# The y images of half 0 in blocks of 16 rows and whole PSUM banks

## The chip, the cores and the metric

The kernel runs on one core of one Trainium2 chip. The metric is device time in microseconds. Before the change the median of three runs is 2890.63 us (2888.65 to 2894.42). A shorter time is better. The profile shown below is of one execution with a span of 2892.8 us.

## The reference

The program has two layers. Layer 0 is a row attention over a 256 x 256 image of 128 channels; its result x1 lies in DRAM. Layer 1 treats the 256 x 128 slices as tokens of a Fourier operator with attention. What matters here is one step of layer 1: the attention output y, a weighted sum over all tokens plus an inverse Fourier image of some modes, followed by an instance norm.

```python
attn = jnp.einsum('bats,basi->bati', probs, vh)
...
attn = fno_layer(attn, p_wr, p_wi, p_bias, p_sw, p_sb, (H, W))
attn = instance_norm(attn + tokens, attn_norm_w, attn_norm_b)
```

There are 256 tokens (two halves of 128, one token to a partition), each an image of 256 rows by 128 columns. In the kernel, y for one half is a matrix of 256 x 128 weights applied to x1 (the skip part, which has attention and identity folded into it), plus the image of the modes, scaled by a constant. The instance norm needs mean and variance over each token's whole image.

## The kernel before, in words

After the attention modes have been worked out, their intermediate `Gd0` lies in DRAM. The stage concerned here starts at 1904.5 us. The generator `y_blocks(a, psum, lo, hi)` at L1308 makes y of half `a` in units of 8 rows, 32 units to a half. Half 0 runs by itself (L1796) with eight PSUM banks; half 1 runs afterwards, woven into other work with four banks. One unit `u` does this:

- **Loads on SyncE's DMA queue.** `load(u + 2)` loads the x1 rows of the unit after next, as one tile `xt` (128 partitions x 2 x 1024 floats, two DMAs of 512 KB, L998). There are three `xt` buffers. If `u` is even it also loads the modes `gs` of a 16-row block (four DMAs of 64 KB, L1229); there are three `gs` buffers. So in the queue the modes of a block stand two units ahead of their use.
- **Skip matmuls on TensorE, L1332.** Four banks, one for each turn `j`, with two accumulating matmuls each: 128 x 128 weights `mpT` against 256 columns of `xt`. A matmul of the code shows as two MATMUL instructions in the profile, so a unit has 16.
- **Image matmuls on TensorE, L1200**, in the helper `image`. For each of two rows and each `j`, a matmul with 32 contraction rows of `gs` against `bsy`, accumulating in the same banks: 8 in the code, 16 in the profile.
- **VectorE.** Four TENSOR_TENSOR (L1342) scale the banks into `blocks`, the SBUF copy of half 0, then two BATCH_NORM_STATS2 (L1344) add the statistics.

A unit uses 256 of a bank's 512 columns, and a pool of eight banks holds two units. The order on the engines is the order of the program text: the stage stands under a manual schedule for the compute engines and SyncE. SyncE is first in, first out: a DMA whose buffer is not yet free holds up every DMA behind it. The three `xt` loads for units 0 to 2 are issued long before the stage.

```python
for j in range(4):
    for sc in range(2):
        nc.tensor.matmul(
            rows_of(ps[j]), mpT[:, sc, tt], by_turn(xt[:, sc])[:, j],
            start=(sc == 0), stop=False,
        )
image(ps, gs[b], bsy, range(2 * s, 2 * s + 2))
```

When half 0 is complete, `psy` is given back and the pool `pz` takes the banks; the norm of half 0 (bn_aggr at L1432) starts from the statistics, and half 1 begins with its own units.

Of the kernel before, what the change touches and what calls it, by code (L numbers as in the profile page):

```python
# [18 lines left out]
P = 128  # L19
# [493 lines left out]
def layer1(tc, I, C, ident, x1d, upool, U, stats2, mv2, out):  # L513
# [9 lines left out]
    with ExitStack() as ctx:  # L523
# [668 lines left out]
        def rows_of(ps):  # L1192
            return ps.rearrange("p (n w) -> p n w", w=W)
# [49 lines left out]
        def run(stage):  # L1243
            for _ in stage:
                pass
# [62 lines left out]
        def y_blocks(a, psum, lo, hi, kept=16):  # L1308

            tt = slice(a * P, (a + 1) * P)  # L1310
            gs = {}

            def load(u):
                if (a, u) not in xts:
                    xts[a, u] = load_x1(a, u)
                if u % 2 == 0:
                    gs[u // 2] = xp.tile([P, 4, P], FP, tag="gs", name=f"gs_{a}_{u}", bufs=3)
                    load_modes(gs[u // 2], Gd0, u // 2, tt)

            load(lo)  # L1320
            load(lo + 1)
            yield 0.0
            for u in range(lo, hi):
                b, s = u // 2, u % 2
                if u + 2 < hi:
                    load(u + 2)
                xt = xts.pop((a, u))
                ps = [psum.pool.tile([P, 512], FP, tag=psum.tag, name=f"yps_{a}_{u}_{j}") for j in range(4)]
                ps = [z[:, 0:256] for z in ps]
# [7 lines that stand above are left out]
                if a == 0:  # L1337
                    yt = blocks[:, b, s * HB : (s + 1) * HB]
                else:
                    yt = xp.tile([P, HB], FP, tag="yt", name=f"yt_{u}")  # L1340
                for j in range(4):
                    nc.vector.tensor_tensor(by_turn(yt)[:, j], rows_of(ps[j]), bc(rwb, 1, 2), ALU.mult)  # L1342
                for g in range(2):
                    nc.vector.bn_stats(ystat[:, a, 2 * u + g, :], yt[:, g * 512 : (g + 1) * 512])  # L1344
                if a:
                    nc.gpsimd.dma_start(ydv[:, a, u * HB : (u + 1) * HB], yt)  # L1346
                yield 4.2

        def mix_modes(mk, acc, F, l, tag, cs):

            T, G, n = P, P // 4, len(cs)
            cs = slice(cs[0], cs[0] + n)
            steps = [
                (i, x, r, dst) for i in range(4)
                for x, r, dst in ((0, "r", 0), (1, "n", 0), (0, "i", 1), (1, "r", 1))
            ]

            of = 4 // n  # L1360

            def products(k):
                made = mk("m", [P, 4, G, 4], f"{tag}m_{cs.start}_{k}")
                for q in range(of):
                    i, x, r, dst = steps[k + q]
                    f = F[:, cs, x, :].rearrange("p c (g i) -> p c g i", i=4)[:, :, :, i]
                    w = mixw[r][:, cs, 16 * l + 4 * i : 16 * l + 4 * i + 4]
                    (nc.gpsimd if (k + q) % 3 == 2 else nc.vector).tensor_tensor(
                        made[:, q * n : (q + 1) * n], bc(f, 3, 4), bc(w, 2, G), ALU.mult
                    )  # L1370
                return made.rearrange("p c g o -> p (c g o)")

            made = products(0)
            for k in range(0, 16, of):
                now = made
                if k + of < 16:
                    made = products(k + of)
                yield 0.6
                for q in range(of):
                    i, x, r, dst = steps[k + q]  # L1380
                    nc.tensor.matmul(  # L1381
                        acc[dst][:, cs.start * T : cs.stop * T], ident, now[:, q * n * T : (q + 1) * n * T],
                        start=(i == 0 and x == 0), stop=(i == 3 and x == 1),
                    )
# [408 lines left out]

        with tc.manual_schedule(engines=COMPUTE | {ENG.SP}):
            with tc.tile_pool(name="psy", bufs=8, space=PSUM) as psy:
                run(y_blocks(0, Banks(psy, "y"), 0, 32))  # L1796
            pz = _Held(tc.tile_pool(name="pz", bufs=4, space=PSUM))
            bq, br = Banks(pz.pool, "q"), Banks(pz.pool, "r")

            def tiles(wp):  # L1800
                return Tiles(F=(wp, "F", 1), f=(wp, "f", 1), m=(wp, "m", 2))

            with yctx:
                U1 = 24
                with tc.tile_pool(name="mp0", bufs=1) as wp:
                    y1 = y_blocks(1, br, 0, U1)
                    weave((2.4 * t for t in first_modes(0, wp, tiles(wp), bq, [(wp, "gt", 1)])), y1)
                    run(y1)
                with tc.tile_pool(name="hp0", bufs=2) as wp:
                    run(first_images(0, wp, xp, bq, br))  # L1810
                with tc.tile_pool(name="mp1", bufs=1) as wp:
                    y1 = y_blocks(1, br, U1, 32)
                    next(y1)
                    m0 = second_modes(
                        0, wp, tiles(wp), bq, [(xp, "xt", 3)], [(wp, "gt", 1)] * 3 + [(xp, "xt", 3)]
                    )
                    weave((2.4 * next(m0) for _ in range(3)), y1)
                    run(y1)
                    m1 = first_modes(
                        1, wp, Tiles(F=(xp, "yt", 2), f=(xp, "yt", 2), m=(xp, "gs", 3)), br, [(xp, "xt", 3)]  # L1820
                    )
                    next(m1)
                    for k, _ in enumerate(iter(lambda: next(m0), None)):
                        if k % 4 == 3:
                            next(m1)
                    for _ in m0:
                        next(m1, None)
                    o0 = output_0(bq)
                    next(o0)
                    y2 = wp.tile([P, NB], FP, tag="gt", name="y2_0", bufs=1)  # L1830
                    nc.sync.dma_start(y2, ydv[:, 1, 0:NB])
                    run(m1)
                    g2 = wp.tile([P, 4, P], FP, tag="m", name="gs2_1_0", bufs=2)
                    next(o0)
                    load_modes(g2, halves[1].Gd1, 0)
                    next(o0)
                with tc.tile_pool(name="hp1", bufs=2) as hp:
                    next(o0)
                    next(o0)
                    due, begun = 0.0, False  # L1840
                    for done in first_images(1, hp, xp, bq, br, ([y2[:, 0:HB], y2[:, HB:]], g2)):
                        if not done:
                            due += 0.9
                            begun = due > 0
                        if begun:
                            next(o0, None)
                        if done and begun:
                            due -= 1.0
                    run(o0)
            pz.release_now()  # L1850
            with tc.tile_pool(name="op1", bufs=2, side="right") as op:
                o1 = Output1(op)
                with tc.tile_pool(name="mp3", bufs=1) as wp, tc.tile_pool(
                    name="mpq3", bufs=8, space=PSUM
                ) as psq:
                    m1 = second_modes(1, wp, tiles(wp), Banks(psq, "q"), [(wp, "gt", 2)], [(wp, "gt", 2)] * 4)
                    next(m1)
                    o1.more = op
                    ahead = o1.ahead()
                    next(ahead)  # L1860
                    next(ahead)
                    next(m1)
                    next(m1)
                    next(ahead)
                    next(ahead)
                    run(iter(lambda: next(m1), 1.2))
                    run(ahead)
                    run(m1)
                with tc.tile_pool(name="opk1", bufs=8, space=PSUM) as psk, tc.tile_pool(
                    name="op2", bufs=1  # L1870
                ) as more:
                    o1.run(Banks(psk, "k"), more)
# [163 lines left out]
```

## Time and profile before

| what | value |
|---|---|
| median time | 2890.63 us |
| span of the profile | 2892.8 us |
| y of half 0 | 1904.5 to 2042.4 us |
| PE / DVE / ACT / POOL busy, whole span | 92 / 69 / 52 / 58 % |
| granted TensorE clock, whole span | 0.952 |
| L1332 `yps<-xt,mpT`, both halves | 1024 instructions, 242.9 us |
| `xt<-x1d` | 128 DMAs of 512 KB |
| `gs<-Gd` | 384 DMAs of 64 KB |

Busy time on PE is the sum of the matmuls' modelled durations; PEld is the weight loads, which overlap it; SPq is SyncE issuing DMAs. In the answers to queries, a row of windows gives length, then the busy time and instruction count of each engine, the granted TensorE clock (1.00 is full), the busy share of the DMA engines, and the bytes moved per second. A timeline row gives start, duration, engine, line, operation, tile, count, and in brackets how long the engine was idle before it and what ended the idling.

### The profile page before, as it was taken

The page shows a single profiled execution, that of the slowest core. Times are in us where ns is not written, and L with a number is a line of the kernel's source. Part 1 is how long each engine was busy: PE and PEld are TensorE (multiplying, and loading weights), DVE is VectorE, ACT ScalarE, POOL GpSimd, SP SyncE. Part 2 cuts the span into 40 slices and gives each one's busy share as a digit, 9 for nine tenths or more (in the row PEclk, how much of TensorE's full clock was granted, in tenths as well). Part 3 has the DMA queues.
Part 4 walks back from the last instruction along what each step waited for, and adds up shares of the span by engine and source line. Part 5 has one row for each costly group of instructions (what it writes and reads, how often), then busy time and mean ns, then how long its engine had stood idle before and what let it go on. Part 6 is the DMA issues. An engine that isn't in the chain of part 4 may idle for free. (4 is left out here: it accounts for less than half of the span.)

```text
span 2892.8 us, 71476 instructions
## 1 busy us (share of the span) xinstructions
PE 2653.2 (92%) x29116; PEld 1940.4 (67%) x29116; DVE 2008.2 (69%) x3263; ACT 1490.7 (52%) x2849; POOL 1682.0 (58%) x1308
## 2 busy tenths in 40 slices
PE   6799999999999999999999899999889988799654
PEld 6677777777777777777777656778665555555533
DVE  7788888888888888888888744756655545365545
ACT  0477777777777777777777622200004611365132
POOL 0399999999999999999999800200114733111211
PEclk9999999999999999999999989999999999799865
DMA  9422222222222222222222101088879983898599
GB/s 362 169 67 67 67 67 67 67 67 67 67 67 67 68 68 68 69 66 72 67 67 67 41 18 53 30 274 276 279 247 313 308 301 131 256 355 303 184 353 344
DMA packets 246705, 430.12 MB, mean 149 GB/s; under 512 B 26278, under 2 KB 174201, under 8 KB 239976
## 3 DMA queue, kind: packets, MB, share of 16 engines
q1 hardware_dynamic: 206568, 335.34, 35.2%
q0 software_dynamic: 22912, 81.80, 7.4%
q10 hardware_dynamic: 16896, 8.39, 1.0%
q8 instruction: 231, 3.78, 0.6%
q14 instruction: 98, 0.80, 0.1%
HBM read 290.17 MB, written 135.27 MB: 147 GB/s over the span
## 5 line engine op out<-in xcount | busy, mean ns | idle before, releaser
L299 POOL TENSOR_TENSOR e<-e,b1T 128x1024 f32<-128x1024 f32 x256 | 607.0, 2371 | 164.3 <-PE u L348 88.8
L303 POOL TENSOR_TENSOR es<-e 128x512 f32<-128x512 f32 x512 | 639.9, 1271 | 20.1
L281 ACT ACTIVATE sc<-sc,b2T 128x512 f32<-128x512 f32 x512 | 339.0, 662 | 365.9 <-PE sc L272 357.6
L323 DVE RECIPROCAL av<-av 128x256 f32<-128x256 f32 x256 | 452.3, 1767 | 27.2 <-DVE og L322 1.4
L281 ACT ACTIVATE e<-sc,b2T 128x512 f32<-128x512 f32 x512 | 348.7, 681 | 0.0
L294 DVE TENSOR_TENSOR e<-sc,b1T 128x1024 f32<-128x1024 f32 x256 | 310.8, 1214 | 0.0
L272 PE MATMUL sc<-qkT 32*128 32x256 f32 x4096 | 294.4, 401 | 1.3 <-DVE e L294 1.3
L311 PE MATMUL av<-e,v 128*32 128x256 f32 x4096 | 274.7, 385 | 0.5 <-POOL e L299 0.5
L1332 PE MATMUL yps<-xt,mpT 128*128 128x256 f32 x1024 | 242.9, 390 | 20.2 <-DVE yt L1342 9.3
L272 PEld LDWEIGHTS sc<-qkT 32*128 32x128 f32 x4096 | 185.6, 184 | 112.4 <-issue 97.8
L322 DVE SCALAR_TENSOR_TENSOR og<-gate,av 128x256 f32<-128x256 f32 x256 | 107.7, 421 | 191.0 <-PE av L316 191.0
L1332 PEld LDWEIGHTS yps<-xt,mpT 128*128 128x128 f32 x1024 | 192.1, 192 | 58.0 <-DVE yt L1342 12.7
L1346 POOL DMA_DIRECT2D yd<-yt x32 | 17.8, 556 | 345.8 <-DVE yt L1342 345.8
L327 POOL TENSOR_TENSOR x<-xt,bo 128x256 f32<-128x256 f32 x256 | 188.0, 734 | 0.0
L246 PE MATMUL qk<-xnT,wT_wq 128*128 128x256 f32 x512 | 179.5, 432 | 1.7 <-ACT xnT L238 1.7
L252 PEld LDWEIGHTS gv<-wT_wv,kvT 128*128 128x128 f32 x1024 | 155.0, 192 | 13.4
L316 PE MATMUL av<-es,ones 128*32 128x256 f32 x2048 | 157.5, 379 | 2.6 <-POOL es L303 2.5
L333 PE MATMUL wo<-wT_wo,og 128*128 128x128 f32 x1024 | 156.8, 276 | 2.7 <-DVE og L324 2.7
L311 PEld LDWEIGHTS av<-e,v 128*32 128x32 f32 x4096 | 107.0, 109 | 76.1 <-POOL e L299 1.0
L348 PE MATMUL u<-adft,x 128*128 128x129 f32 x1024 | 156.4, 275 | 0.0
L258 DVE COPY v<-gv 128x256 f32<-128x256 f32 x256 | 108.6, 424 | 68.6 <-PE gv L256 68.6
L252 PE MATMUL gv<-wT_wv,kvT 128*128 128x128 f32 x1024 | 156.0, 275 | 0.0
(546 smaller groups left out, 5282.2 us busy)
## 6 DMA issues: line engine op xcount, KB each, us to landing
xt<-x1d SPq DMA_DIRECT2D x128, 512.0 KB
xb<-in_x_dram SPq DMA_DIRECT2D x32, 1024.0 KB
xt<-in_x_dram SPq DMA_DIRECT2D x128, 256.0 KB
kt<-in_L_conv_kv_x_dram SPq DMA_DIRECT2D x128, 256.0 KB
x1d<-x SPq DMA_DIRECT2D x256, 128.0 KB
y<-yd SPq DMA_DIRECT2D x62, 512.0 KB
gs<-Gd SPq DMA_DIRECT2D x384, 64.0 KB
yd<-yt POOLq DMA_DIRECT2D x32, 512.0 KB, 6.2
```

Of the source, the lines that this page charges most:

```text
L246: nc.tensor.matmul(ps[:, 0:256], wT["wq"], xnT, start=True, stop=True)
L252: nc.tensor.matmul(ps[:, 256 + c * P : 256 + (c + 1) * P], kvT[:, c * P : (c + 1) * P], wT["wv"], start=True, stop=True,)
L272: nc.tensor.matmul(sc[h // 2][:, h % 2, c * 256 : (c + 1) * 256], qkT[p, 256 + c * P : 256 + (c + 1) * P], qkT[p, 0:256], start=True, stop ...
L281: nc.scalar.activation(r["e"][1][:, :, c, :] if hp else z, z, AF.Exp, bias=b2T[:, c, s : s + 1])
L294: nc.vector.tensor_tensor(r["e"][0].rearrange("p h c q -> p (h c q)"), r.pop("sc").rearrange("p h x -> p (h x)"), b1T[:, 0:2].rearrange("p ...
L299: nc.gpsimd.tensor_tensor(e1, e1, b1T[:, 2:4].rearrange("p h c q -> p (h c q)"), ALU.mult)
L303: nc.gpsimd.tensor_tensor(r["es"][hp], e[:, :, 0, :], e[:, :, 1, :], ALU.add)
L311: nc.tensor.matmul(ps[hd, 0:256], r["v"][:, c, hd], r["e"][h // 2][:, h % 2, c, :], start=(c == 0), stop=(c == 1),)
L316: nc.tensor.matmul(ps[32 * h : 32 * h + 32, 256:512], self.ones, r["es"][h // 2][:, h % 2, :], start=True, stop=True,)
L323: nc.vector.reciprocal(rd, rd)
L327: nc.gpsimd.tensor_tensor(r["x1"], r["x"], bc(self.bo, 1, 2), ALU.add)
L1332: nc.tensor.matmul(rows_of(ps[j]), mpT[:, sc, tt], by_turn(xt[:, sc])[:, j], start=(sc == 0), stop=False,)
```

## The change

Half 0 gets a function of its own, `y_half_0`. It works in 16 blocks of 16 rows. A block takes four whole banks of 512 columns; the skip matmuls of its first unit fill the first half of each bank and those of its second unit the other half, and only the first of them carries the start flag. Then all four rows' image matmuls follow at once. VectorE scales a whole bank with one TENSOR_TENSOR of 512 columns. This is meant to need fewer and larger instructions on VectorE, and fewer changes between the two kinds of matmul. At the top of a block come the loads: first `xt` of the units 2b+2 and 2b+3, then `gs` of block b itself. Half 1 stays as it was.

```diff
+        def y_half_0(psum):
+
+            tt = slice(0, P)
+            for b in range(16):
+                for u in (2 * b + 2, 2 * b + 3) if b else (0, 1, 2, 3):
+                    if u < 32 and (0, u) not in xts:
+                        xts[0, u] = load_x1(0, u)
+                gs = xp.tile([P, 4, P], FP, tag="gs", name=f"gs_0_{b}", bufs=3)
+                load_modes(gs, Gd0, b, tt)
+                ps = [psum.tile(f"yps_0_{b}_{j}") for j in range(4)]
+                for s in range(2):
+                    xt = xts.pop((0, 2 * b + s))
+                    for j in range(4):
+                        for sc in range(2):
+                            nc.tensor.matmul(
+                                rows_of(ps[j])[:, 2 * s : 2 * s + 2], mpT[:, sc, tt], by_turn(xt[:, sc])[:, j],
+                                start=(s == 0 and sc == 0), stop=False,
+                            )
+                image(ps, gs, bsy)
+                for j in range(4):
+                    nc.vector.tensor_tensor(by_turn(hb[b])[:, j], rows_of(ps[j]), bc(rwb, 1, 4), ALU.mult)
+                for g in range(4):
+                    nc.vector.bn_stats(ystat[:, 0, 4 * b + g, :], hb[b][:, g * 512 : (g + 1) * 512])
...
             with tc.tile_pool(name="psy", bufs=8, space=PSUM) as psy:
-                run(y_blocks(0, Banks(psy, "y"), 0, 32))
+                y_half_0(Banks(psy, "y"))
```

## The prediction

> **What bounds the kernel now.** I read the page for the whole, then the busy time of the engines in the window of this stage, then the timeline, then SyncE's own timeline. The window first (columns: length; busy time of PE, PEld, DVE, ACT, POOL; clock; DMA share; GB/s):
>
> ```profile
> 1904.50:2042.40 137.90, 137.88 (x1024) 111.79 (x1024) 84.27 (x188) 0.00 (x0) 0.00 (x0) 1.00 0.88 278
> ```
>
> TensorE is busy for all 137.9 us at full clock; VectorE has 84.3 us of work, and the DMA engines are 88% busy. So TensorE sets the pace: 137.9 / 32 = 4.31 us a unit, 8.62 us a 16-row block. The timeline of one unit:
>
> ```profile
> 1917.42 3.72 PE L1332 MATMUL yps<-xt,mpT 128*128 128x256 f32 x16
> 1917.51 1.41 DVE L1342 TENSOR_TENSOR blocks<-yps,rwb 128x256 f32<-128x256 f32 x4 [1.57 <-PE yps L1200]
> 1918.95 1.29 DVE L1344 BATCH_NORM_STATS2 ystat<-blocks 128x6 f32<-128x512 f32 x2
> 1921.07 0.73 PE L1200 MATMUL yps<-bsy,gs 32*128 32x128 f32 x16
> 1921.72 3.72 PE L1332 MATMUL yps<-xt,mpT 128*128 128x256 f32 x16
> ```
>
> From start to start, the skip part takes 1921.07 - 1917.42 = 3.65 us and the image part 0.65 us. VectorE works 2.7 us of 4.3 and waits for TensorE. SyncE's queue over the first units:
>
> ```profile
> 1908.25 5.11 SPq L998 DMA_DIRECT2D xt<-x1d  x4
> 1913.40 1.85 SPq L1229 DMA_DIRECT2D gs<-Gd  x4
> 1916.86 5.11 SPq L998 DMA_DIRECT2D xt<-x1d  x4
> 1922.02 1.85 SPq L1229 DMA_DIRECT2D gs<-Gd  x4
> ```
>
> An `xt` load goes out when its buffer's skip matmuls end: 1904.52 to 1908.25 is 3.73 us after a unit's start, and 1913.11 to 1916.86 is 3.75. The x4 row hides a wait for the next buffer in its middle. The modes issued at 1913.40 are first used at 1925.38, 12 us later. This slack is why no DMA wait appears on TensorE here.
>
> How long a load takes I read from the trace's completion records of the DMAs. The `xt` pair issued from 1912.55 was complete at 1917.96 (5.4 us), and the four `gs` behind it, issued from 1913.40, at 1919.01: 6.46 us after the `xt` pair's first issue. The next such pair gives 1921.17 to 1927.56, 6.39 us.
>
> [...] `gs` completes 1.05 us after that `xt`.
>
> [...]
>
> ```profile
> 2118.50:2121.40 2.90, 0.00 (x0) 0.03 (x1) 2.69 (x7) 0.60 (x1) 0.60 (x1) 1.00 0.98 394
> 2122.40:2125.80 3.40, 3.40 (x82) 2.80 (x67) 1.29 (x2) 1.07 (x2) 0.00 (x0) 0.50 0.03 6
> 2126.00:2130.00 4.00, 3.50 (x30) 2.72 (x28) 0.57 (x2) 0.00 (x0) 1.52 (x2) 1.00 0.88 241
> ```
>
> TensorE was idle for 2.94 us, and 1.0 us after it resumed it ran 3.4 us at clock 0.50. A gap of 2.58 us ending at 2154.59 was followed by 0.50 from 2156.5, one of 2.57 us ending at 2319.21 by 0.50 from 2320.4. Gaps of 1.55 us (one each 8.7 us between 2084 and 2112) brought none.
>
> [...]
>
> **The change part by part.** Call T the start of a block's first skip matmul.
>
> TensorE's instructions are the same in number and shape (32 skip, 32 image MATMULs a block). There is one change from image to skip instead of two. Image matmuls of 32 in a row take 1.10 us elsewhere (L1200 into `ups`), against 2 x 0.65 = 1.3 here: at most 0.2 us a block, 3 us in all. I take 1.3 and count the gain as nothing.
>
> VectorE: eight TENSOR_TENSOR of 256 columns, 8 x 0.415 = 3.3 us a block, become four of 512. [...] this trace has 415 ns for 256 columns, and for 512 columns from PSUM (`Fy`, L1173) 0.69 us. So 4 x 0.69 = 2.8 us, a saving of 0.5 us a block or 9 us in all. With 2.6 us of statistics that makes 5.4 us of work in a block of over 8.6: it lies beside TensorE's work and is worth nothing. PSUM still holds two blocks; a block's banks are free long before the next but one.
>
> The loads are what counts. In block b SyncE has, in this order: `xt` 2b+2, `xt` 2b+3, `gs` b. There are three `xt` buffers, so 2b+3 takes that of 2b, which block b itself reads first. It can't be issued before T + 3.75, and `gs` b stands behind it, though its own buffer is free. Behind `gs` stand the next loads, with slack: `xt` 2b+4 waits for unit 2b+1 in any case. The image matmuls wait for `gs` b on TensorE, and all later blocks are queued behind them.
>
> - `gs` complete: T + 3.75 + L. L was 6.46 and 6.39 us with the DMA engines still at the previous load. Here they are idle by then (`xt` 2b+2 went out at the end of the preceding block's skip matmuls, some 5 us before T). I take 6.2. Lower bound: 4.5, that is 0.83 us to issue the `xt` pair, 1.85 for four `gs`, and about 1.8 for the last to land, with nothing in front. Upper bound: 7.2, from the slowest `xt` pair (issued 1908.25, complete 1914.39, 6.14) and 1.05 for `gs`.
> - Skip matmuls end at T + 7.3. TensorE idles until T + 9.95: a gap of 2.65 us.
> - Image: 1.3 us. Period: 3.75 + 6.2 + 1.3 = 11.25 us against 8.62, so 2.63 more.
> - Clock: a gap of 2.65 us is in the region where half clock followed. 3.4 us at half speed lose 1.7 us; they fall on image and first skip matmuls, ahead of the release on which the next `gs` hangs, so they lengthen the period. With some gaps that don't trip it I take 1.5: 12.75 us.
>
> Block 0 has no gap before it: 11.25. Blocks 1 to 14: 14 x 12.75 = 178.5. In block 15 no `xt` is left to load, so `gs` 15 follows `gs` 14 directly and is early: 7.3 + 1.3 + 1.5 = 10.1. Sum 199.9 us against 137.9: 62.0 more.
>
> Handing over: half 1's first skip matmul waited 1.49 us for the last four TENSOR_TENSOR (row at 2043.89); with 2.8 instead of 1.4 us of them, 1.4 more. Everything after needs half 0's statistics or TensorE, so it moves as a whole. Together +63.4: 2890.6 + 63.4 = 2954.0 us.
>
> **The rivals.**
>
> - *Wait without the clock.* [...] Then 15 x 2.63 + 1.4 = +41: 2932 us. For it: gaps near 1.5 us trip nothing, and my gap is under 3. Against: all three gaps near 2.6 to 2.9 us above did.
> - *Short wait.* `gs` slips past `xt` and L is 4.5: period 9.55, gap 0.95, no half clock; 15 x 0.93 + 1.4 = +15: 2906 us. Against it: `gs` completed after `xt` both times.
> - *No wait.* `gs` arrives by T + 7.3. Then only the saved 0.2 us x 16 and the hand-over remain: -3.2 + 1.4 = -2, 2889 us: not slower. Only if the 3.75 us before the release is not there, for which nothing speaks: the queue's waits in this stage are all of `xt` on the skip matmuls.
> - *Longer.* L = 7.2 with a full 1.7 us of half clock: 13.95 a block, 15 x 5.3 + 1.4 = +81: 2972 us; two windows at half clock would add some more.
>
> **How the numbers follow.** Wait with half clock 0.56 (2954), wait alone 0.24 (2932), longer 0.10 (2972), short wait 0.06 (2906), no wait 0.04 (2889). The range from 2912 to 2978 us takes in the first three with the bounds of L. Slower by over 0.2% (5.8 us) is all but the last: 0.95; within 0.2%: 0.03; faster: 0.02.
>
> **What would show it.** In the profile after: TensorE before L1200 `yps` waits for DMA `gs<-Gd`, some 2.65 us, 15 times; a period of 11 to 13 us; DMA share down from 0.88 to near 0.6; a mean clock in the stage near 0.85. The TENSOR_TENSOR rows at 0.69 us with longer idle before them. If `gs` is issued at the top of a block rather than after its first unit, or TensorE is still fully busy, the argument is wrong. If the gap is there and the clock is 1.00, it is the first rival.

## The result, and the profile after

The changed kernel takes 2958.5 us (median of 6 runs), against 2892.53 us for the kernel before on the same chip: ratio 1.0227, 95% interval 1.0212 to 1.0242. That is 66 us slower. The forecast was 2954.

First the window of the stage, with the same columns as for the kernel before:

```profile
1901.30:2103.90 202.60, 165.37 (x1024) 138.12 (x1024) 74.79 (x122) 0.00 (x0) 0.00 (x0) 0.89 0.60 190
```

The stage lasts 202.6 us instead of 137.9, with the same 1024 matmuls: one start flag to a bank added none. TensorE is idle for 37.2 us of it, and what it does takes 27.5 us longer, at a mean clock of 0.89. The DMA share has fallen from 0.88 to 0.60. VectorE has 9.5 us less to do, which shortens nothing here. The timeline of block 1:

```profile
1913.37 8.38 PE L1363 MATMUL yps<-xt,mpT 128*128 128x256 f32 x32
1919.17 1.85 SPq L1229 DMA_DIRECT2D gs<-Gd  x4
1923.97 1.99 PE L1200 MATMUL yps<-bsy,gs 32*128 32x128 f32 x32 [2.23 <-DMA gs<-Gd]
1925.80 2.49 DVE L1369 TENSOR_TENSOR blocks<-yps,rwb 128x512 f32<-128x512 f32 x4 [7.59 <-PE yps L1200]
1925.90 8.86 PE L1363 MATMUL yps<-xt,mpT 128*128 128x256 f32 x32
```

Both signs that the prediction named are there. The modes go out at 1919.17, nearly six microseconds into their own block. TensorE finishes its skip matmuls and waits for them, 2.23 us here. And the skip matmuls take 8.38 and 8.86 us, where blocks at full clock show 7.17 in the same trace (the block that starts at 1939.10, for one). SyncE's own rows:

```profile
1908.48 10.65 SPq L998 DMA_DIRECT2D xt<-x1d  x4
1919.17 1.85 SPq L1229 DMA_DIRECT2D gs<-Gd  x4
1921.78 10.36 SPq L998 DMA_DIRECT2D xt<-x1d  x4
1932.18 1.85 SPq L1229 DMA_DIRECT2D gs<-Gd  x4
```

A row of four `xt` DMAs, two pairs, used to span 5.11 us and now spans over 10: between the first pair and the second SyncE stands still until the block's first unit has released its buffer, and the modes follow only then. Over the stage and a little of what follows, the sum of the waits (who waited for whom; total, times, longest):

```profile
PE yps L1200 <- DMA gs<-Gd: 37.2, 15, 3.3
```

There are fifteen waits, one in each of blocks 0 to 14 and none in block 15, whose modes follow those of block 14 without an `xt` between. The clock, in windows from the wait of block 1 on (packets are counted where they start, so the DMA share of a short window can come out above 1):

```profile
1922.00:1924.00 2.00, 0.03 (x1) 0.03 (x1) 0.00 (x0) 0.00 (x0) 0.00 (x0) 1.00 1.05 279
1924.00:1926.00 2.00, 2.00 (x33) 1.86 (x33) 0.20 (x1) 0.00 (x0) 0.00 (x0) 1.00 1.01 381
1926.10:1929.40 3.30, 3.30 (x9) 2.55 (x9) 3.27 (x6) 0.00 (x0) 0.00 (x0) 0.50 0.12 46
1929.60:1934.50 4.90, 4.90 (x24) 4.19 (x23) 1.19 (x3) 0.00 (x0) 0.00 (x0) 1.00 0.45 130
```

While it waits the clock still shows 1.00. The price comes later, here two microseconds after work has resumed: 3.4 us at 0.50, in the next block's first unit (9 matmuls in 3.3 us, where 24 take 4.9). The clock records have 13 such windows in the stage, after 11 of the 15 waits; two waits were followed by two windows each.

### The profile page after: what moved, and what is told of

Same layout as the page of the kernel before. It is cut to its first block, busy times and chain, and to the rows that moved or that the text cites. A ratio compares the mean times of both kernels' runs of the same rounds, so it can differ in the third digit from the quotient of the medians.

```text
span 2956.7 us, 71398 instructions
## 1 busy us (share of the span) xinstructions
PE 2681.0 (91%) x29116; PEld 1966.4 (67%) x29116; DVE 2001.5 (68%) x3199; ACT 1490.5 (50%) x2849; POOL 1680.3 (57%) x1308
## 5 line engine op out<-in xcount | busy, mean ns | idle before, releaser
L1723 ACT ACTIVATE blocks<-h2ps,col 128x512 f32<-128x512 f32 x128 | 88.9, 778 | 129.9 <-PE h2ps L1200 129.9
L256 PE MATMUL gv<-xnT,wT_wg 128*128 128x256 f32 x512 | 153.4, 381 | 0.0
```

## The experiments

The theory: in SyncE's queue the modes of a block stand behind an `xt` load that cannot go out before that same block's first unit is done, and the wait that follows also costs half clock. The rival: whole banks and images of 16 rows at once cost by themselves. All variants start from the changed kernel. Each ratio is to the kernel before on the same chip; the first four variants ran on one chip and the last four on another, so variants of the two groups are compared by ratios and by their traces.

**Modes first.**

```diff
             for b in range(16):
+                gs = xp.tile([P, 4, P], FP, tag="gs", name=f"gs_0_{b}", bufs=3)
+                load_modes(gs, Gd0, b, tt)
                 for u in (2 * b + 2, 2 * b + 3) if b else (0, 1, 2, 3):
...
-                gs = xp.tile([P, 4, P], FP, tag="gs", name=f"gs_0_{b}", bufs=3)
-                load_modes(gs, Gd0, b, tt)
```

> The changed kernel with one thing undone: in a block of half 0 the four loads of its modes come ahead of its two xt loads in SyncE's queue instead of behind them. Theory (the modes stand behind an xt load that waits for the block's own first unit): the modes go out a block earlier and land long before use, no wait of TensorE for them, a period of 8.4 to 8.6 us, clock 1.00 in the stage. 16 x (-0.2) + 1.1 for the hand-over: 2887 to 2892 us, within 0.2% of before. Rival (whole banks, or images of 16 rows at once, cost by themselves): the time stays above 2930 us.

Measured: 2886.7 us, ratio 0.9981 (0.9972 to 0.9991). Moving two lines takes back the whole loss and a little more than the band expected. The stage without its hand-over, and a block in it:

```profile
1901.90:2033.20 131.30, 131.30 (x1024) 111.65 (x1024) 74.74 (x122) 0.00 (x0) 0.00 (x0) 1.00 0.88 285
```

```profile
1910.07 7.17 PE L1363 MATMUL yps<-xt,mpT 128*128 128x256 f32 x32
1917.18 1.17 PE L1200 MATMUL yps<-bsy,gs 32*128 32x128 f32 x32
1918.28 7.17 PE L1363 MATMUL yps<-xt,mpT 128*128 128x256 f32 x32
```

In this window TensorE is never idle, and a block takes 8.21 us, 0.41 less than the 8.62 of before. So the blocks do bring something, and the rival falls. From start to start the skip part is 7.11 us instead of 2 x 3.65, the image part 1.10 instead of 2 x 0.65: half of the gain lies on each side of the change between the two kinds of matmul. The hand-over to half 1 costs some of it again. In the kernel before, then here:

```profile
2043.89 3.72 PE L1332 MATMUL yps<-xt,mpT 128*128 128x256 f32 x16 [1.49 <-DVE blocks L1342]
```

```profile
2033.27 2.48 DVE L1369 TENSOR_TENSOR blocks<-yps,rwb 128x512 f32<-128x512 f32 x4 [3.22 <-PE yps L1200]
2035.81 5.41 PE L1332 MATMUL yps<-xt,mpT 128*128 128x256 f32 x16 [2.56 <-DVE blocks L1369]
```

The first unit of half 1 waits 2.56 us instead of 1.49, and its matmuls then take 5.41 us instead of 3.72; the clock records have one window of 3.41 us at half clock there, from 2036.0.

**Small units, late modes.** Units of 8 rows with half-filled banks as before, but the load order of the changed kernel.

```diff
                 for s in range(2):
                     xt = xts.pop((0, 2 * b + s))
+                    ps = [psum.tile(f"yps_0_{b}_{s}_{j}")[:, 0:256] for j in range(4)]
...
-                image(ps, gs, bsy)
+                    image(ps, gs, bsy, range(2 * s, 2 * s + 2))
...
```

> The opposite half of the change: the 8-row units, half-filled banks and 256-column TENSOR_TENSOR of the kernel before, but the load order of the changed one (both xt, then the block's own modes). Theory: the first image now comes after one unit of skip matmuls instead of two, so the gap is longer by a unit, some 6 us in each block; period 3.75 + 6.5 + 0.8 + 3.65 + 0.65 = 15.3 us and 1.7 to 3.4 us more for half clock: 15 x (6.7 to 10.1) = 100 to 150 us slower than before, 2990 to 3040 us, worse than the changed kernel. Rival (the large blocks cost): it returns to about 2892 us.

Measured: 3015.57 us, ratio 1.0426 (1.04 to 1.0452). The order of the loads alone, without any large block, costs 123 us, the half clock that follows its waits included (here a unit's skip matmuls take 3.69 us before the first wait and 5.45 us after it).

```profile
1898.25 3.69 PE L1363 MATMUL yps<-xt,mpT 128*128 128x256 f32 x16 [0.30 <-issue]
1907.46 1.90 PE L1200 MATMUL yps<-bsy,gs 32*128 32x128 f32 x16 [5.52 <-DMA gs<-Gd]
1909.29 5.45 PE L1363 MATMUL yps<-xt,mpT 128*128 128x256 f32 x16
```

The wait is some 3 us longer than in the changed kernel: there the second unit's skip matmuls lie between the release and the first image matmuls, here no skip matmuls do. Large blocks therefore soften the wrong order.

**Modes on another queue.** The text order stays as in the changed kernel, but ScalarE issues the modes.

```diff
-                load_modes(gs, Gd0, b, tt)
+                for j in range(4):
+                    nc.scalar.dma_start(gs[32 * j : 32 * j + 32], Gd0[:, j, 4 * b : 4 * b + 4, tt])
```

> The changed kernel with the modes of half 0 issued from ScalarE's DMA queue instead of SyncE's; order in the text, sizes and buffers stay. Theory (head-of-line blocking in SyncE's queue, not the time of the transfer): ScalarE has no work in this stage, so the modes go out as soon as one of three buffers is free, up to two blocks early; no wait, 2887 to 2892 us. Rival (the transfers compete for the DMA engines, and the modes are slow wherever they are issued): waits of a microsecond and more on gs remain, over 2910 us.

Measured: 2884.39 us, ratio 0.9971 (0.996 to 0.9982). The stage again takes 131.3 us with TensorE busy throughout:

```profile
1904.50:2035.80 131.30, 131.30 (x1024) 111.64 (x1024) 74.73 (x122) 1.28 (x1) 0.00 (x0) 1.00 0.87 287
```

The same bytes move at the same DMA share of 0.87. So it is not that the DMA engines are too slow for them; it is the place in SyncE's queue. The time lies a little under the band, which counted 0.2 us a block where 0.41 is gained.

**The gap filled.** Five matmuls with zero weights between skip and image matmuls add zero to the banks and keep TensorE busy while it would wait.

```diff
+            zeros = sp.tile([P, P], FP, name="zeros")
+            nc.vector.memset(zeros, 0.0)
...
+                for k in range(5 if b < 15 else 0):
+                    nc.tensor.matmul(
+                        ps[k % 4][:, 0:256], zeros, mpT[:, 0, :], start=False, stop=False
+                    )
                 image(ps, gs, bsy)
```

> The changed kernel, and between the skip and the image matmuls of blocks 0 to 14 five more matmuls of 256 columns with zero weights (they add zero): 5 x 0.456 = 2.3 us of TensorE work, about the length of its wait. Theory (part of the loss is the half clock that the gaps set off, 11 windows of 3.4 us in the profile of the changed kernel): TensorE is never idle for over 1 us, the clock stays at 1.00, and the stage is 11 to 13 x 1.5 = 16 to 20 us shorter although it has more work: 2936 to 2944 us. Rival (the half clock falls where TensorE would wait anyway): unchanged or a little slower, 2955 to 2965 us.

Measured: 2934.25 us, ratio 1.0137 (1.0113 to 1.0161), a little below the band. The kernel with 15% more matmuls in the stage is faster than the changed one, by 24 us in the medians and 26 by the ratios.

```profile
1901.10:2080.20 179.10, 175.65 (x1174) 150.86 (x1174) 74.75 (x122) 0.00 (x0) 0.00 (x0) 1.00 0.65 215
```

```profile
1958.55 7.17 PE L1365 MATMUL yps<-xt,mpT 128*128 128x256 f32 x32
1965.56 2.32 PE L1370 MATMUL yps<-mpT,zeros 128*128 128x256 f32 x10
1967.81 1.73 PE L1200 MATMUL yps<-bsy,gs 32*128 32x128 f32 x32
```

The clock stays at 1.00 and a typical block takes 11.1 us. The stage is 23.5 us shorter than the 202.6 us of the changed kernel; 13 windows of 3.41 us at half speed make 22.2. So the three lengths split the loss: 131.3 us with the modes first, 47.8 more for the wait alone (179.1, with whatever the filling itself delays), 23.5 more with the half clock (202.6).

**VectorE in small pieces.** Modes first, but eight TENSOR_TENSOR of 256 columns a block instead of four of 512; the statistics of the first half of the block stand between the two groups of four.

```diff
...
-                    nc.vector.tensor_tensor(by_turn(hb[b])[:, j], rows_of(ps[j]), bc(rwb, 1, 4), ALU.mult)
+                        nc.vector.tensor_tensor(
+                            by_turn(yt)[:, j], rows_of(ps[j])[:, 2 * s : 2 * s + 2], bc(rwb, 1, 2), ALU.mult
+                        )
...
```

> The kernel with the modes ahead of the xt loads and blocks of 16 rows, but VectorE reads each bank in two TENSOR_TENSOR of 256 columns, eight a block, as before. Theory (VectorE's saving is worth nothing inside the stage; the gain of 0.41 us a block seen with the modes first comes from TensorE's one change of kind instead of two): the period stays 8.21 us; only the hand-over is longer, since the last TENSOR_TENSOR ends 4.6 us after the last image instead of 2.5: 2888 to 2890 us, ratio 0.998 to 0.9995. Rival (the gain comes from the larger VectorE instructions): the period goes back towards 8.62 us and the time to 2893 us or more.

Measured: 2891.89 us, ratio 1.0003 (0.9989 to 1.0016), just above the band expected. The period stays at 8.21 us in its trace, so none of the 0.41 us comes from VectorE. What differs in the trace is the hand-over:

```profile
2037.95 6.29 PE L1332 MATMUL yps<-xt,mpT 128*128 128x256 f32 x16 [4.17 <-issue]
```

The trace names nothing that ended the wait, but the last four TENSOR_TENSOR, from 2036.45 to 2037.85, end just before it does. Half 1's first unit waits 4.17 us instead of 2.56, and its matmuls take 6.29 us instead of 5.41: 2.5 us in all; the clock records have two windows at half clock there instead of one. The rest of the difference to modes first is within the intervals.

**Small units in the last block.** Modes first, and block 15 in two units of 8 rows as in the kernel before.

```diff
+                if b < 15:
...
+                    continue
+                for s in range(2):
...
+                    image(ps, gs, bsy, range(2 * s, 2 * s + 2))
...
```

> Modes ahead of the xt loads, blocks 0 to 14 of 16 rows, block 15 as two units of 8 rows as before. Theory (the hand-over costs 1.07 us of longer wait and 1.68 us of half clock that the wait of 2.56 us sets off): the wait returns to 1.5 us, no half clock at half 1's first unit, 0.4 us lost in block 15: 2.3 us less than with modes first alone, ratio 0.997 to 0.998, about 2884 us. Rival (half 1 has slack that hides its first unit's delay): the same as with modes first alone, 0.998.

Measured: 2881.33 us, ratio 0.997 (0.9959 to 0.9981), about 9 us better than the kernel before and the lowest ratio here, though not clear of its neighbours.

```profile
2037.61 3.72 PE L1332 MATMUL yps<-xt,mpT 128*128 128x256 f32 x16 [1.49 <-DVE blocks L1386]
```

The wait is back at 1.49 us and the matmuls at 3.72: what the hand-over had cost is gone in the trace. In the times the step from 0.9981 to 0.997 has the size expected, but the intervals overlap.

**Modes between the two `xt` loads.**

```diff
                 for u in (2 * b + 2, 2 * b + 3) if b else (0, 1, 2, 3):
+                    if u == 2 * b + 3:
+                        load_modes(gs, Gd0, b, tt)
                     if u < 32 and (0, u) not in xts:
                         xts[0, u] = load_x1(0, u)
...
-                load_modes(gs, Gd0, b, tt)
```

> The changed kernel with the block's modes between its two xt loads: behind xt 2b+2, which waits for the end of the preceding block's skip matmuls, and ahead of xt 2b+3, which waits for the block's own first unit. Theory (it is the wait of xt 2b+3 alone that holds the modes up): they go out some 0.8 us after the preceding block's skip matmuls end, land 6.5 us after that xt, some 1.6 us before they are needed: no wait of TensorE, period 8.2 us, ratio 0.997 to 0.999. Rival (any megabyte ahead of the modes in the same block costs, since their transfer is slow): waits on gs remain and the time is above 2900 us.

Measured: 2888.33 us, ratio 0.9998 (0.9987 to 1.001), just above the band. One megabyte ahead of the modes does no harm here, where that load does not wait for the same block: all blocks but one take 8.2 us with no wait. The margin is small, though. The one shows

```profile
2017.39 0.29 PEld L1200 LDWEIGHTS yps<-bsy,gs 32*128 32x128 f32 x2 [0.47 <-DMA gs<-Gd]
2017.39 2.08 PE L1200 MATMUL yps<-bsy,gs 32*128 32x128 f32 x32
2017.97 1.32 PEld L1200 LDWEIGHTS yps<-bsy,gs 32*128 32x128 f32 x30 [0.29 <-DMA gs<-Gd]
```

and takes 9.26 us: the weight loads wait for the modes twice, and the image part takes 2.0 us instead of 1.1, so its last modes came about a microsecond too late. In its trace the stage is only 1 us longer than with modes first; the rest of the 1.7 thousandths between the two ratios this stage does not explain, and the intervals overlap.

**Both together.** ScalarE's queue and the small units in block 15.

```diff
-                load_modes(gs, Gd0, b, tt)
...
+                for j in range(4):
+                    nc.scalar.dma_start(gs[32 * j : 32 * j + 32], Gd0[:, j, 4 * b : 4 * b + 4, tt])
+                if b < 15:
...
```

> Candidate for the fastest: modes from ScalarE's DMA queue, blocks 0 to 14 of 16 rows, block 15 as two units of 8 rows. Both parts' gains add if they are independent: 2.3 us less than with the ScalarE queue alone, about 2882 us, ratio 0.996 to 0.9975. If the gain of the ScalarE queue over modes first came from the hand-over itself, it is the same as the variant with modes first and the last block by 8 rows.

Measured: 2885.86 us, ratio 0.9978 (0.9966 to 0.9989), just above the band. The times show no gain over either part alone. In the trace both parts are there: the blocks of 16 rows take 8.21 us, half 1's first unit waits 1.49 us and its matmuls take 3.72. A difference of 2 us is too small for these times, whose intervals all overlap; they cannot rank the variants at 0.997 to 0.998, nor ScalarE's queue against SyncE's.

## Why the prediction was right

**The order of the loads.** Right, in mechanism and place: `xt` 2b+3 waits for unit 2b, the modes stand behind it, TensorE waits. Undoing the order alone takes the loss away; making it alone costs 123 us.

**The landing, L.** A little too small: 6.2 us was taken. By the completion records the last of the four `gs` came 6.2 to 6.8 us after the first `xt` issue in 12 blocks and 7.2 to 7.8 in the other three, 6.68 on average. That the idle DMA engines would make it shorter than the 6.4 us seen before was wrong. The 1.8 us in its lower bound, for a load with nothing in front, agrees with the kernel before: five `gs` issued from 1901.26 to 1903.61, with no `xt` in front, were complete 1.5 to 1.9 us after the end of their issue.

**The gap and the image part.** The gap was put at 2.65 us and was 37.2 / 15 = 2.48. It is shorter although L is longer, because the four `gs` land one after another, some 0.3 us apart, and the first image matmuls start with the first of them. In exchange the image part takes 1.8 to 3.1 us instead of the 1.3 predicted, the longest partly at half clock. Here the sum treated four loads as one.

**The half clock.** Right in kind and nearly in size: 1.5 us was taken for each of 15 blocks, 22.5 us, and the filled gap shows 23.5. That the size fits is in part luck: eleven waits set it off instead of nearly all, but two did so for two windows. Of two waits of 2.27 us one set it off and one did not, one of 2.34 passed and one of 2.07 did not: the length alone does not decide. The mean clock "near 0.85" does not follow from the prediction's own sum: 22.5 us lost in 199.9 gives 0.89, which is what was measured.

**The period.** 12.75 us was predicted for blocks 1 to 14; from the start of block 1 (1913.37) to that of block 15 (2095.62) it was 182.25 / 14 = 13.0. The stage was put at 199.9 us and took 202.6. That they agree so well is luck in one respect. Blocks 0 to 14 took 12.95 us on average. Without any wait a block takes 8.21 (modes first) instead of the 8.6 assumed. The half clock adds 22.2 / 15 = 1.5 and the gap 2.5; the remaining 0.8 is image matmuls that wait for the later `gs`. So the wait costs about 3.3 us a block, where 2.65 was taken (the filled gap gives 47.8 / 15 = 3.2), and the change of kind, below, gives 0.4 back. The two errors nearly cancel.

**The change of kind on TensorE.** Too small by half: "at most 0.2 us a block, 3 us in all", counted as nothing. With the order repaired it is 0.41 us a block, 6.6 us in all, since the skip part gains as much as the image part; only the image part was looked at. In the rival without a wait this and the hand-over (1.1 and 1.7 us, see below) would have made 2890.6 - 6.6 + 2.8 = 2886.8 us rather than the 2889 given.

**VectorE.** Right: 0.68 us for 512 columns in the trace against 0.69 taken, hidden throughout, and splitting the instructions does not change the period.

**The hand-over.** The longer wait was 2.56 us against 1.49, so 1.1 and not 1.4 us more. What the sum left out is that this wait too can set off the half clock: 1.7 us more in the first unit. Both numbers are the same in the trace of the changed kernel. Stage and hand-over together are there 64.7 + 2.8 = 67.5 us longer, against 66 us in the times: within their noise the rest of the program moves as a whole, as predicted.

**The rivals.** The wait without the clock (2932 us) is near what the filled gap measured, 2934 us, with the same two errors cancelling in it; it was not what happened. The others fell: every gap was 2.0 us or more, there was a wait in each of the 15 blocks, and the mean landing was not 7.2 us but 6.68.

## What to carry to other kernels

In SyncE's queue each load inherited here the wait of the loads ahead of it: the modes of block 1, whose own buffer was free, went out 5.8 us into their block, 0.85 us after the `xt` that had waited. Where a loop body's loads are written together for such a queue, ask for each what releases its buffer, and put those that wait for the present iteration last. A short wait of TensorE in every iteration can cost half as much again by the clock it loses afterwards (here 23.5 us on top of 47.8); filling the gap with matmuls that add zero shows whether that is so.

## What the runs showed of the hardware that was not expected

- TensorE fell to half clock in this stage after 11 of 15 waits, of 2.07 to 3.34 us, always for whole windows of 3.41 us, starting from 0.1 us before to 2.1 us after work had resumed; after the other four, of 2.00 to 2.34 us, it did not fall. The kernel before has a wait of 2.19 us, from 2202.48, with such a window from 2204.32. All the starts in the stage lie on one grid of 3.41 us (1912.42 and 1926.08, 13.65 us apart, are four windows). But where a gap falls on this grid does not settle it either. The grid cuts the wait of 2.23 us in block 1 into 0.91 and 1.31, and the clock fell; it cuts that of 2.00 us in block 14 into 1.68 and 0.32, and the clock did not. What decides stays open; no run moved a gap against the grid.
- Passing from 128-row skip matmuls to 32-row image matmuls and back costs TensorE 0.41 us a pair here, about 0.2 us in each direction, although no engine waits for another. VectorE is ruled out as the cause by a run. That it is the change of kind is argued from where the time falls: the whole banks and the single start flag came together with it, and no run parts them.
